# Two layers on a graph in one kernel: the 2 KB vector `bm` is fetched from ACT's queue at the start

## The chip, the cores and the metric

The kernel runs on one core of one Trainium2 chip. The metric is the device time of one execution in microseconds (us), as a median over runs. The kernel before took 2413.67 us (three runs, 2409.06 to 2415.69).

A core has five engines, each with its own instruction stream that is worked through in order: PE (TensorE, matrix products), DVE (VectorE), ACT (ScalarE), POOL (GpSimd) and SP (SyncE, which only issues transfers here). ACT and POOL issue transfers too. An instruction that needs another engine's result, or a transfer's data, waits on a semaphore, and all that stands behind it on its engine waits as well.

## The reference

The input `x` is 32 batches of 512 channels (C) by 1024 nodes (N), in float32; `adj` is a 512 x 512 matrix. Two layers follow one another, each on a normalized input:

```python
h = relu(layernorm(x))                  # over the 1024 nodes of a row
q, k = wq . h, wk . h                   # one number a node
scores[m, n] = leaky(q[n] + k[m])       # slope 0.01 below zero
att = softmax(scores) over n
x = x + relu(adj @ (h @ att.T) + bm)    # bm: 512 numbers, one a channel
h = relu(layernorm(x))
x = x + (h.T @ (adj*adj)).T + bias      # bias: 1024 numbers, one a node
```

`bm` is added to each channel of the first layer's output before its relu.

## The kernel before, in words

**Work.** A batch is held as four tiles of 128 channels x 1024 nodes (`c` = 0 to 3). The N x N attention is never built: since a score is a sum of two numbers behind a leaky slope, the nodes are sorted by `q`, and each row of the softmax becomes a sum of a prefix and a suffix of the sorted values. So for each batch:

- `load` (line 301, SP) brings `x`; `stats` (314, 315, DVE), `norm` (319, ACT), `slopes` (323, 325, DVE) and `relu` (332, ACT) normalize it.
- `scores` (344, PE, copied by ACT in 349) gives `q` and `k`; they go to DRAM and come back broadcast to all partitions as `qrow` (351, 353, SP).
- `rank` (384 to 393, DVE) and `lower` (400, ACT) count for each node how many are smaller; `to_rows` (420 to 426, DVE) makes row numbers `idx` of it.
- `value` (447, PE) is `pv` = `h` times the transposed `adj` (`wmT`), copied to `v` by ACT in `spread` (454); `scatter` (459, 460, POOL) writes each node's row of `v` to its sorted place in a DRAM table `td`.
- `fetch` (477, SP) reads the sorted table back as `vs`, after all scatters of the batch have landed. `weights` (486, 489, ACT), `later` (497, 501, DVE), `totals` (509 to 514, PE and DVE) and `stationary` (520, POOL) make the masks `sm`; `scan` (530, PE) and `sums` (540 to 547, ACT and SP) build prefix and suffix sums and write them to `td`.
- `gather` (552, POOL), `excess`, `divide`, `weigh` (577) and `combine` (581, DVE) take each node's sums; `turn` (588 on PE, 590 on DVE) transposes them and adds them into the reloaded `x`. Here `nbm`, which is -`bm`, is used: max(value, -`bm`) plus the residual. `bm` itself is added later, in `finish` (603).
- the second layer: statistics again, `lift` (338, adds `bias`), `propagate` (595, PE, `pg`) and `finish`.

**Order.** All these steps are listed with a due time each (the tables `PLAN`, `FIRST` and `LAST`), sorted by it, and written out in that order. The order on each engine is therefore fixed by the program, and steps of several batches interleave; batches 0 to 4 at the start have times of their own.

**Around the change.** Ahead of the steps stand constants: `wq` and `wk` are begun on ACT's queue (lines 222 and 223), and ACT computes a first square root, `root` (227). The step `biases` has three instructions: the transfer of `bm` (257) and of `bias` (258) on SP, and `nbm` on DVE (259). The step `pads` clears a tile on DVE (263, 264) and writes it to two places of each of the five tables, 20 transfers on SP (267, 268). A pair's second transfer overlaps the first in one row of the table, and so waits until the first has landed.

On SP, in order: eight `x` loads and `adj`, then batch 0's `qd` and `qrow`, one load, the 20 pads, two loads, `bm`, `bias`, one load, the six transfers of batch 0's fetch, batch 1's `qd` and `qrow`. On DVE, in order: statistics of batches 0 and 1, the ranks of batch 0 (with the pads' clearing among them), `nbm`, a tile's statistics, batch 1's slopes, batch 0's factors. The first reader of `nbm` after that is batch 0's `turn`, at 225.6 us; `bm_sb` is first used in `finish`, at 283.7 us.

A transfer issued from SP or ACT takes the next of eight completion semaphores, in turn, and waits for the transfer that had it last.

Of the kernel before, what the change touches and what calls it, by code (L numbers as in the profile page):

```python
# [16 lines left out]
P = 128  # L17
# [140 lines left out]
def kernel(  # L158
# [32 lines left out]
    nc = tc.nc  # L191
# [34 lines left out]
    root = const.tile([P, 1], F32, name="root")  # L226
    nc.scalar.activation(root, eps_sb, AF.Sqrt)
    bm_sb = const.tile([P, NC], F32, name="bm_sb")
    nbm = const.tile([P, NC], F32, name="nbm")
    bias_sb = const.tile([P, N], F32, name="bias_sb")  # L230
    before = const.tile([P, P], F32, name="before")
# [22 lines left out]
        nc.gpsimd.tensor_tensor(wsq, s.adj, s.adj, ALU.mult)  # L254

    def biases(s):
        nc.sync.dma_start(bm_sb, bm.rearrange("(c p) -> p c", p=P))
        nc.sync.dma_start(bias_sb, bias.partition_broadcast(P))
        nc.vector.tensor_scalar(nbm, bm_sb, -1.0, None, ALU.mult)

# [365 lines left out]
    for b in range(B):  # L626
        s = Batch()
        s.b, s.pv, s.v, s.sm, s.pt, s.pg = b, {}, {}, {}, {}, {}
        s.x, s.idx, s.vs, s.vt, s.sc = {}, {}, [], [], []
        if b == 0:  # L630
            for f in (
                adjacency, turn_adjacency, square, biases, pads, compare_mask, masks,
            ):
                plan(s, f, f.__name__, args=((),))
        for f in (
            load, reload, lift, rank, lower, value, spread, scatter, to_rows, scan, sums, gather,
            weigh,
        ):
            plan(s, f, f.__name__)
        for f in (  # L640
            scores, columns, factors, from_rows, fetch, weights, later, totals, excess, divide,
        ):
            plan(s, f, f.__name__, args=((),))
        for l in range(2):
            plan(s, norm, f"norm{l}", l, args=((),))
            plan(s, slopes, f"slopes{l}", l, args=((),))
            plan(s, stats, f"stats{l}", l)
            plan(s, relu, f"relu{l}", l)
        for i in range(NH):
            plan(s, turn, f"turn{i}", i)  # L650
        plan(s, stationary, "stationary", args=((0,), (3,), (6,)))
        for f in (propagate, finish):
            plan(s, f, f.__name__, args=all_of(NC, range(NH)))
        plan(s, combine, "combine", args=all_of(NN, (1, 2)))
# [31 lines left out]
```

## Time and profile before

| | us |
|---|---|
| median of three runs | 2413.67 |
| the profiled execution | 2400.17 |
| its span, first to last instruction | 2398.5 |
| PE busy in the span | 2305.7 (96%) |
| DVE busy | 1936.4 (81%) |
| ACT busy | 1585.2 (66%) |
| POOL busy | 723.7 (30%) |
| PE busy in the first 130 us | 90.9 |
| PE busy from 400 to 1000 us | 600.0 |

How to read it: a profile is of one execution, so a sum made from it is set against that execution's time. PE's matrix products are pipelined, and a busy PE may still run at half clock; the granted clock is given by stretch, 1.00 being full. In a list of waits the columns are the instruction that waited, what it waited for, then us in total, the number of times, and the longest. In a list in order of time they are the start in us, the duration in us, engine, line, operation, what is written <- what is read, shapes, the number of instructions that were merged, and in brackets the idle time of the engine just before with what ended it. A row by stretch has from:to and its length, then for PE, weight loads, DVE, ACT and POOL the busy us and the number of instructions, then the granted clock, the busy share of the 16 DMA engines, and GB/s. `SPq` and `ACTq` stand for an engine that issues a transfer.

### The profile page before, as it was taken

Reading aid. Unit: us, or ns where it says so; the run is one execution under the profiler, and the core shown is the slowest. Engines: PE = TensorE matmul, PEld = TensorE weight load, DVE = VectorE, ACT = ScalarE, POOL = GpSimd, SP = SyncE. Lnnn points to the kernel's source line nnn. Section 1 sums busy time; section 2 is a strip of 40 time slices with the busy share of each in tenths; the row PEclk is TensorE's granted clock in tenths of the full one; section 3 lists DMA queues with packets and bytes.
Section 4 is the critical chain, followed back from the end, with each engine's and each line's share of the span. In section 5 each row is a group of like instructions: output and inputs, shape, how many; then the busy total and the mean of one; then the engine's idle time right before and its main releaser. Section 6 shows DMA issues by size and latency. Waiting matters only on the chain.

```text
span 2398.5 us, 28425 instructions
## 1 busy us (share of the span) xinstructions
PE 2305.7 (96%) x7632; PEld 1004.9 (42%) x7632; DVE 1936.4 (81%) x5008; ACT 1585.2 (66%) x2880; POOL 723.7 (30%) x973
## 2 busy tenths in 40 slices
PE   5787999999999999999999999999999999999897
PEld 2233344444444444444444444444444444444343
DVE  5548878888888888888888888888898888888775
ACT  3666677667766767776766776676777766667541
POOL 2213332323442232333233233223233324223210
PEclk9898999999999999999999999999999999999999
DMA  5679879988889988988988888898898897888972
GB/s 163 183 184 281 275 251 299 283 268 274 309 258 299 302 257 270 304 284 273 299 274 251 300 298 272 285 301 253 273 309 280 276 299 243 266 282 275 286 294 97
DMA packets 206916, 643.49 MB, mean 268 GB/s; under 512 B 29130, under 2 KB 29258, under 8 KB 206756
## 3 DMA queue, kind: packets, MB, share of 16 engines
q1 hardware_dynamic: 148356, 372.68, 53.5%
q0 software_dynamic: 57344, 268.99, 30.0%
q8 instruction: 62, 1.02, 0.2%
q14 instruction: 98, 0.80, 0.1%
q10 hardware_dynamic: 1056, 0.00, 0.0%
HBM read 429.94 MB, written 211.62 MB: 267 GB/s over the span
## 4 chain that ended last, share of the span: by engine, by line
PE 87%; DMA 6%; DVE 2%; ACT 2%; issue 1%; SPq 1%; POOL 1%; POOLq 0%; DVEq 0%; ACTq 0%
PE pg L595 35%; PE pv L447 34%; PE sc L530 12%; PE tr L588 4%; DMA vs<-td 2%; PE pq L344 2%; DVE g L581 1%; DMA td<-pad 1%; DMA x<-in_x_dram 1%; DMA g<-td,idg 1%; DMA qd<-qr 0%; POOL g L552 0%; ACT junk L400 0%; SPq L477 0%; ACT t L543 0%
## 5 line engine op out<-in xcount | busy, mean ns | idle before, releaser
L447 PE MATMUL pv<-wmT,x 128*128 128x512 f32 x2048 | 907.0, 598 | 20.0 <-ACT x L332 20.0
L595 PE MATMUL pg<-h,wsq 128*128 128x512 f32 x2048 | 913.3, 598 | 10.6 <-ACT h L332 10.6
L447 PEld LDWEIGHTS pv<-wmT,x 128*128 128x128 f32 x2048 | 382.5, 191 | 511.7 <-issue 437.4
L595 PEld LDWEIGHTS pg<-h,wsq 128*128 128x128 f32 x2048 | 379.1, 190 | 509.6 <-issue 467.7
L520 POOL TENSOR_TENSOR sm<-mask_a,wc 128x192 f32<-128x192 f32 x96 | 49.4, 515 | 1283.8 <-DVE wc L497 815.5
L530 PE MATMUL sc<-vs,sm 128*64 128x512 f32 x1152 | 322.8, 629 | 38.7 <-POOL sm L520 17.2
L581 DVE SCALAR_TENSOR_TENSOR g<-g,cf 128x512 f32<-128x512 f32 x512 | 347.7, 746 | 12.4 <-ACT g L577 12.4
L460 POOL DMA_INDIRECT td<-v,idx x256 | 292.3, 1142 | 146.8 <-POOL v L459 49.8
L400 ACT ACTIVATE junk<-qrow,qk 128x1024 bf16<-128x1024 f32 x256 | 294.4, 1150 | 6.9 <-DMA qrow<-qd 5.1
L552 POOL DMA_INDIRECT g<-td,idg x256 | 243.1, 950 | 143.3 <-issue 71.5
L540 ACT COPY vs<-sc 1x512 f32<-1x512 f32 x256 | 145.4, 568 | 185.9 <-PE sc L530 185.7
L590 DVE SCALAR_TENSOR_TENSOR y<-tr,nbm,y 128x512 f32<-128x512 f32 x256 | 174.4, 743 | 97.2 <-PE tr L588 80.5
L603 DVE SCALAR_TENSOR_TENSOR y<-pg,bm_sb,y 128x512 f32<-128x512 f32 x256 | 187.9, 739 | 45.7 <-PE pg L595 45.4
L543 ACT COPY t<-sc 128x512 f32<-128x512 f32 x288 | 168.0, 583 | 74.1 <-DMA td<-t 69.0
L389 DVE TENSOR_SCALAR_CACHE_REDUCE junk<-qrow,qk,cnt 128x896 bf16<-128x896 f32 (+6 forms) x224 | 180.3, 805 | 8.2
L384 DVE TENSOR_SCALAR_CACHE_REDUCE junk<-qrow,qk 128x128 bf16<-128x128 f32 (+6 forms) x224 | 165.5, 739 | 14.0 <-DMA qrow<-qd 9.2
L530 PEld LDWEIGHTS sc<-vs,sm 128*64 128x64 f32 x1152 | 77.3, 139 | 231.9 <-issue 90.4
L314 DVE BATCH_NORM_STATS2 st<-x 128x6 f32<-128x512 f32 x256 | 162.9, 677 | 10.5 <-DMA x<-in_x_dram 10.5
L577 ACT ACTIVATE g<-g,cf 128x512 f32<-128x512 f32 x256 | 163.5, 712 | 6.4 <-DVE cf L571 6.4
L332 ACT ACTIVATE x<-x,nmr,rstd 128x1024 f32<-128x1024 f32 x128 | 148.5, 1233 | 25.8 <-DVE nmr L325 25.4
L338 DVE TENSOR_TENSOR y<-y,bias_sb 128x1024 f32<-128x1024 f32 x128 | 154.5, 1225 | 8.4 <-ACT h L332 8.4
L314 DVE BATCH_NORM_STATS2 st<-y 128x6 f32<-128x512 f32 x256 | 159.0, 663 | 0.0
(109 smaller groups left out, 1931.3 us busy)
## 6 DMA issues: line engine op xcount, KB each, us to landing
vs<-td SPq DMA_DIRECT2D x192, 384.8 KB
td<-t SPq DMA_DIRECT2D x576, 128.2 KB
x<-in_x_dram SPq DMA_DIRECT2D x128, 512.0 KB
y<-in_x_dram SPq DMA_DIRECT2D x128, 512.0 KB
out_dram<-y SPq DMA_DIRECT2D x128, 512.0 KB
qrow<-qd SPq DMA_DIRECT2D x32, 512.0 KB
td<-v,idx POOLq DMA_INDIRECT x256, 7.2
g<-td,idg POOLq DMA_INDIRECT x256, 11.4
```

The lines of the kernel that those rows point to most:

```text
L314: nc.vector.bn_stats(st[:, i, :], s.x[c][:, ts(i, HALF)])
L389: nc.vector.tensor_scalar(junk[:, j * P :], s.qrow[:, j * P :], qc, first, ALU.is_lt, ALU.add, accum_out=s.cnt[:, 1, j : j + 1],)
L400: nc.scalar.activation(junk, s.qrow, AF.Sign, bias=s.qk[:, 1, j : j + 1], accum_out=s.sgn[:, j : j + 1])
L447: nc.tensor.matmul(pv, s.h[c][:, ts(j, P)], wmT[:, c, :], start=(c == 0), stop=(c == NC - 1))
L460: i = nc.gpsimd.indirect_dma_start(tds[s.b % TABLES][:, :], bass.IndirectOffsetOnAxis(ap=s.idx[j // 4][:, j % 4 : j % 4 + 1], axis=0), v[: ...
L530: nc.tensor.matmul(p[ts(k, HP), :], s.sm[i][k], s.vs[h][:, 0:C], start=True, stop=True)
L543: nc.scalar.copy(t[:, 0:C], p)
L552: nc.gpsimd.indirect_dma_start(s.g[:, j, :], None, tds[s.b % TABLES][0 : 3 * NB * HP, :].rearrange("(s k) w -> s (k w)", k=3), bass.Indire ...
L581: nc.vector.scalar_tensor_tensor(r, s.g[:, j, k * W : k * W + C], s.cf[:, k, j : j + 1], r, ALU.mult, ALU.add)
L590: nc.vector.scalar_tensor_tensor(xh, pt, nbm[:, o : o + 1], xh, ALU.max, ALU.add)
L595: nc.tensor.matmul(pg, wsq[:, r, ts(c, P)], s.h[r][:, ts(i, HALF)], start=(r == 0), stop=(r == NC - 1),)
L603: nc.vector.scalar_tensor_tensor(xh, s.pg.pop((c, i)), bm_sb[:, c : c + 1], xh, ALU.add, ALU.add)
```

## The change

The transfer of `bm` is taken out of the step `biases` and begun with the constants, on ACT's queue, behind `root`. Nothing else is changed: `biases` still begins `bias` on SP and computes `nbm` on DVE, at its place in the order.

```diff
     root = const.tile([P, 1], F32, name="root")
     nc.scalar.activation(root, eps_sb, AF.Sqrt)
     bm_sb = const.tile([P, NC], F32, name="bm_sb")
+    nc.scalar.dma_start(bm_sb, bm.rearrange("(c p) -> p c", p=P))
     nbm = const.tile([P, NC], F32, name="nbm")
...
     def biases(s):
-        nc.sync.dma_start(bm_sb, bm.rearrange("(c p) -> p c", p=P))
         nc.sync.dma_start(bias_sb, bias.partition_broadcast(P))
         nc.vector.tensor_scalar(nbm, bm_sb, -1.0, None, ALU.mult)
```

## The prediction

> **What bounds the kernel now.** The page comes first. TensorE (PE) is busy for 2305.7 of 2398.5 us, and the row of forty slices shows where it is not:
>
> ```profile
> PE   5787999999999999999999999999999999999897
> ```
>
> Only the first four slices (240 us) and the last two fall short. I then took the busy time by stretch: from 300 us to 2000 us PE is idle for 1.7 us in all. The steps' order is fixed, so the end can only move if PE's idle time in the ramp moves. The wait that the diff touches lies in that ramp. The view of all that touches `bm_sb`, then the waits between 46 and 90 us:
>
> ```profile
> L259 DVE TENSOR_SCALAR nbm<-bm_sb x1: 169/169/169, 66.4 to 66.4; 128x4 f32<-128x4 f32 x1
>   DMA bm_sb<-in_L_gnn_bm_dram: 19.7, 1
> ```
> ```profile
> POOL sm L520 <- DVE wc L497: 26.9, 1, 26.9
> PE pv L447 <- ACT x L332: 19.8, 1, 19.8
> DVE nbm L259 <- DMA bm_sb<-in_L_gnn_bm_dram: 19.7, 1, 19.7
> ```
>
> VectorE (DVE) stands 19.7 us at `nbm`. Behind it are batch 1's slopes, behind those its relu on ScalarE (ACT), and behind that PE, idle 19.8 us. The tempting forecast is that all this comes back. So I asked for the order of time just after, and what PE meets next:
>
> ```profile
> 78.13 0.55 SPq L351 DMA_DIRECT2D qd<-qr  x1
> 81.62 0.30 ACT L486 ACTIVATE w<-vs,nq 128x3 f32<-128x3 f32 x1 [2.04 <-DMA vs<-td]
> 81.71 1.28 DVE L314 BATCH_NORM_STATS2 st<-x 128x6 f32<-128x512 f32 x2
> 83.15 0.31 DVE L497 TENSOR_SCALAR wc<-w,ident 128x9 f32<-128x9 f32 x2
> 83.88 0.50 POOL L520 TENSOR_TENSOR sm<-mask_b,wc 128x192 f32<-128x192 f32 x1
> 84.88 1.08 PE L530 MATMUL sc<-vs,sm 128*64 128x512 f32 x4
> ```
>
> At 81.62 ACT is waiting for batch 0's fetch (`vs<-td`) from DRAM; its last part sets `w`, then `wc`, `sm`, and PE's first scan matmul. In PE's order only three `pv` groups, the scores and one transpose (69.60 to 84.95) stand between the stall and that scan. The fetch stands on SP behind the pads (34.02 to 60.28), and no part of it waits for `nbm`. It, not the stall, is the later of the two gates.
>
> **What the Trainium skill says.** "DMA: Bandwidth & Descriptors", section "Issuing engines are not separate DMA queues": a transfer begun from another engine runs on the same 16 DMA engines and interleaves; only issue time is saved. The same page, "Queues, rings and completion order": each DMA engine goes round the queue rows packet by packet. The trace agrees on the kind of packet: ACT's queue moved 1056 packets for two 2 KB vectors, one for each 4-byte element and 32 more; and it agrees that they share, since the big loads slow down while they run:
>
> ```profile
> 2.00:7.00 5.00, 0.00 (x0) 0.00 (x0) 1.99 (x5) 1.49 (x2) 0.68 (x3) 1.00 0.83 246
> 7.00:13.00 6.00, 1.47 (x7) 1.50 (x8) 2.66 (x7) 0.00 (x0) 0.00 (x0) 1.00 1.04 402
> 10.00:13.00 3.00, 1.47 (x7) 1.50 (x8) 0.51 (x3) 0.00 (x0) 0.00 (x0) 1.00 1.04 415
> 63.00:64.00 1.00, 0.00 (x0) 0.00 (x0) 0.00 (x0) 0.00 (x0) 0.00 (x0) 0.50 1.02 410
> 64.00:66.00 2.00, 0.00 (x0) 0.00 (x0) 0.00 (x0) 0.00 (x0) 0.00 (x0) 0.50 0.89 210
> ```
>
> The last number is GB/s. "TensorE: Matmul & The Clock Gate", section "What's actually happening": PE drops to half clock after an idle window of about 3.4 us and returns after a busy one. Here the granted clock (third from the end) agrees: 0.50 over 57 to 69 and still over 69 to 74, then 0.96:
>
> ```profile
> 57.00:69.00 12.00, 0.00 (x0) 0.00 (x0) 2.49 (x7) 0.69 (x1) 0.00 (x0) 0.50 0.76 230
> 69.00:74.00 5.00, 4.40 (x5) 1.63 (x6) 4.07 (x19) 4.97 (x6) 0.00 (x0) 0.50 1.07 213
> 74.00:78.00 4.00, 4.00 (x37) 1.61 (x36) 0.00 (x0) 0.73 (x2) 0.00 (x0) 0.96 1.07 221
> ```
>
> **The change, part by part.**
>
> Start, added: one transfer of some 528 packets on ACT's queue after `root` (3.65 us). ACT's issue, 0.5 us as for `wq` and `wk`, is free: ACT then stands idle until 14.26. But its packets come while the fourth load of batch 0 is awaited; DVE starts on it at 12.70 after 2.46 us of waiting, and everything up to the pads and the fetch hangs on that. Upper bound: 2 to 7 us moved 246 GB/s against 415, so two such transfers (and the ramp) cost 5 x (1 - 246/415) = 2.0 us, 1.0 each. Lower bound: 7 to 13 us, with the tail of `wk` in it, lost 6 x (1 - 402/415) = 0.2. A gain is excluded: packets are added ahead of the load. I take +0.6.
>
> Start, a new wait: SP's loads of batch 1 wait for `wq` and `wk` already (1.2 and 3.2 us in SP's waits; the last two issue at 6.55 and 10.06), so these transfers share completion semaphores in turn, and `bm` joins the turn. `wk` came 3.5 us after `wq`, so I put `bm` at 13.6, and the last load's issue there too. A load issued at 0.81 was in use at 4.98, so the third load of batch 1, now issued about 10.1, is there by 14.3 (used at 17.72) and the fourth by 17.8 (used at 22.63). What is queued behind on SP, `qd`, issues at 21.85. Cost nothing; without that cover at most 3.5 us.
>
> Middle, removed: SP's issue, 0.43 us plus a gap, 0.47. SP's next issues run without a wait up to the fetch at 63.27, but the data are limited by the DMA engines, so this alone is hidden. What counts is the packets: over 64 to 66 us the engines moved 210 GB/s against 410, so 2 x (1 - 210/410) = -0.98 us for the data behind. Fetch landing: +0.6 - 0.98 = -0.4, from 81.6 to 81.2.
>
> Middle, the stall: DVE goes through `nbm` at 46.76 + 0.6 = 47.4. The relu then waits for ACT's copy of the last `pv` (ends 50.45), so PE starts batch 1 at 50.45 + 0.6 + 1.3 = 52.4, 17.2 us earlier. Its 15.35 us of work are over by about 67, and it waits for the scan. In the new order the statistics at 81.71 are long done, so `wc` follows `w` (82.10 - 0.4) at 81.75, not 83.15: -1.4. The scan needs the second `sm`, done at 84.38 - 1.4 = 83.0, against PE's 84.95: -1.9. That is what is left of 19.7.
>
> After it: the clock. PE has now idled from 67 to 83, so it is cold at the scan and not at 69.60. The cold `pv` group took 6.20 us against 3.70 warm: +2.5. That price moves from a place where PE was to wait anyway to one where PE then works without a break until 103. PE: -1.9 + 2.5 = +0.6. DVE's `den`, 1.36 us behind the scan, now takes 2.7: 83.0 + 2.7 = 85.7, not 86.24, and `qrow` (begun at 81.47 when `qd` has landed, which lies behind the fetch now) moves by some -0.3; so batch 1's ranks begin 0.3 to 0.5 earlier, and with them its scatters. PE's +0.6 reaches SP through `td<-t` (113.75), where the next fetch had 0.4 us to wait; the fetch at 115.00 moves by -0.4 to +0.2. Sum at the end: 0 within 1 us. The profiled execution took 2400.17 us (1.7 outside its span), 13.5 under the median of the runs, 2413.67; I carry the difference, 0, over to the median: 2413.7.
>
> **The rivals.**
>
> 1. The gain goes through: the scan would be ready whenever PE is. PE gains 17.2 us: 2396.5. For it: 19.7 us on DVE and the chain that ended last, which runs through `bm_sb`. Against: ACT's 2.04 us wait for the fetch at 81.62. It needs a fetch 17 us earlier, and SP is at the pads until 60.28. 5 in 100.
>
> 2. The start slips by all of the 3.5 us that a transfer on ACT's queue took: fetch +2.5, scan +1.0, PE +3.5, ranks +2.3; 2416.5. Against: 402 GB/s was kept with small packets present. 8 in 100.
>
> 3. Slower: PE stays cold after the scan. Each us of work at half clock costs half a us, and 2.3 are covered (1.9 and the 0.4 at SP). It decides (over 7.2 us) from 19 us of half clock on. Such a stretch exists: 0.50 over 207.4 to 221 with PE busy 6.26 us of 13.6 and 0.51 to 228. With 20 us: +7.7, 2421.4. Against: behind the scan stand solid `pv` groups (PE busy 15.00 of 15 us from 88 on), and at 69.60 the clock was back in under 5 us. 5 in 100.
>
> **How the numbers follow.** Some 0.3% (7.2 us) is what a measurement of this kernel can tell from no change. The collapse has 80 in 100, with 2411 to 2416.5 as its own range (1 us of the sum and the spread of the runs, 2409 to 2415.7, on a median). Rival 1 is faster, rival 3 slower, rival 2 the same; 2 in 100 are left for what I don't see, and 2 on each side of the collapse for the runs' spread. Faster 0.07, same 0.86, slower 0.07. The range 2408 to 2419.5 takes in the collapse, rival 2 and the spread.
>
> **What would show it.** Right: no wait for `bm` on DVE; PE at batch 1's `pv` by about 52; PE idle some 16 us ahead of the first scan at about 83, with half clock to about 88; a fetch that lands within 1 us of 81.6; PE solid from 300 us as now. Wrong: a fetch landing many us earlier (rival 1), DVE's fourth statistics at 14 or later, not 12.70 (rival 2), half clock beyond 100 us (rival 3). The forecast fails if something outside the ramp moves, such as a DMA order that repeats in each batch; I find none, since from `bias` on the turn of the semaphores is as before.

## The result, and the profile after

| | before | after |
|---|---|---|
| median of 12 runs, us | 2414.10 | 2412.64 |
| lowest and highest, us | 2409.06, 2416.16 | 2408.20, 2417.45 |
| ratio, with its 95% interval | | 0.9999 [0.9989, 1.0008] |
| the profiled execution, us | 2400.17 | 2409.72 |
| its span, us | 2398.5 | 2408.0 |

No difference can be measured: the interval leaves room for 2.7 us of gain and 1.9 us of loss. A stall of 19.7 us is gone from VectorE, and the kernel is not measurably faster. (The ratio is estimated from all runs; it is not the quotient of the two medians.)

The two profiled executions differ by 9.6 us the other way. That says nothing of the change: 28 runs of the kernel before on one chip, made for the experiments below, lay between 2410.79 and 2423.97 us. What a profile can show is the order of events in the ramp.

The page of after, its row of slices for PE, then its row for ACT's DMA queue:

```profile
PE   6787899999999999999999999999999999999797
...
q10 hardware_dynamic: 1584, 0.01, 0.0%
```

The first slice is fuller by a digit, the fifth and the 38th are emptier by one. ACT's queue now moves 1584 packets, not 1056: the 528 of `bm`. The view of all that touches `bm_sb`, the two lines on the transfer and on `nbm` (fastest, median and slowest in ns, then first and last start):

```profile
L229 ACTq DMA_DIRECT2D bm_sb<-in_L_gnn_bm_dram x1: 463/463/463, 0.8 to 0.8; - x1
L259 DVE TENSOR_SCALAR nbm<-bm_sb x1: 160/160/160, 47.0 to 47.0; 128x4 f32<-128x4 f32 x1
```

`nbm` runs at 47.01 without a wait, instead of 66.44 after 19.68. The waits of after between 46 and 90 us (us in total, times, longest):

```profile
POOL sm L520 <- DVE wc L497: 25.2, 1, 25.2
ACT w L486 <- DMA vs<-td: 18.2, 3, 12.8
...
PE sc L530 <- POOL sm L520: 13.7, 1, 13.7
...
DVE wc L497 <- ACT w L486: 8.6, 1, 8.6
...
PE pv L447 <- ACT x L332: 3.9, 2, 2.4
```

PE's wait for the relu fell from 19.8 to 3.9 us, and one of 13.7 us stands in its place, at the first scan. Read upwards, the list is the chain that makes it: the scan waits for `sm`, `sm` for `wc`, `wc` for `w`, and `w` for batch 0's fetch, `vs<-td`. The same chain in order of time, each engine's own list of after:

```profile
53.85 2.26 PE L447 MATMUL pv<-wmT,x 128*128 128x512 f32 x4 [2.36 <-ACT x L332]
...
82.75 2.43 PE L530 MATMUL sc<-vs,sm 128*64 128x512 f32 x4 [13.71 <-POOL sm L520]
...
87.56 14.00 PE L447 MATMUL pv<-wmT,x 128*128 128x512 f32 x32
```
```profile
81.49 0.30 ACT L486 ACTIVATE w<-vs,nq 128x3 f32<-128x3 f32 x1 [2.59 <-DMA vs<-td]
```
```profile
81.83 0.42 DVE L497 TENSOR_SCALAR wc<-w,ident 128x9 f32<-128x9 f32 x2 [8.57 <-ACT w L486]
...
85.55 0.17 DVE L514 COPY den<-pd 128x9 f32<-128x9 f32 x1 [3.20 <-PE pd L510]
86.09 0.34 DVE L384 TENSOR_SCALAR_CACHE_REDUCE junk<-qrow,qk 128x128 bf16<-128x128 f32 x1 [0.37 <-DMA qrow<-qd]
```

PE starts batch 1 at 53.85 instead of 69.60, 15.75 us earlier. But the last part of the fetch reaches `w` at 81.49, where it was 81.62, and so the scan begins at 82.75, only 2.13 us earlier than at 84.88. The scan's first four matmuls take 2.43 us, not 1.08, because PE is cold; the clock by stretch shows it (third number from the end):

```profile
57.00:69.00 12.00, 11.36 (x54) 4.67 (x54) 0.67 (x2) 2.18 (x4) 0.00 (x0) 1.00 0.64 190
69.00:74.00 5.00, 0.04 (x1) 0.00 (x0) 2.42 (x8) 0.00 (x0) 0.00 (x0) 0.91 1.04 282
74.00:78.00 4.00, 0.00 (x0) 0.00 (x0) 0.00 (x0) 0.49 (x2) 0.00 (x0) 0.50 1.08 241
78.00:83.00 5.00, 0.25 (x1) 0.26 (x2) 0.52 (x3) 1.44 (x5) 0.85 (x2) 0.50 0.54 121
83.00:86.00 3.00, 2.67 (x13) 1.60 (x13) 0.17 (x1) 0.76 (x2) 1.22 (x4) 0.50 0.97 291
86.00:90.00 4.00, 4.00 (x10) 1.67 (x11) 3.73 (x11) 3.94 (x8) 0.00 (x0) 0.91 0.34 87
```

The work of 57 to 69 is now done at the full clock, and the half clock has moved to 74 to 86, after the idle stretch (0.04 us of PE work from 69 to 74, none from 74 to 78). PE's unbroken stretch starts at 87.56, where PE's list of before has it at 88.27: 0.7 us are left of 19.7.

```profile
88.27 14.00 PE L447 MATMUL pv<-wmT,x 128*128 128x512 f32 x32
```

That the fetch reaches `w` at the same time is the sum of two movements that cancel. SP's list of before, then of after:

```profile
60.33 1.08 SPq L301 DMA_DIRECT2D x<-in_x_dram  x2
...
63.27 4.64 SPq L477 DMA_DIRECT2D vs<-td  x6
```
```profile
62.81 1.07 SPq L301 DMA_DIRECT2D x<-in_x_dram  x2
...
65.15 3.96 SPq L477 DMA_DIRECT2D vs<-td  x6
```

From the first load behind the pads to `w` it is 21.3 us in before (60.33 to 81.62) and 18.7 in after (62.81 to 81.49). This stretch, with the fetch in it, became 2.6 us shorter, and the pads ended 2.5 us later. The pads' pace varies between executions of one kernel, as the last experiment shows. The stretch behind them varies less: a second profile of before has 21.8 us, and four more profiles with an early `bm`, these pads and nothing added ahead of the fetch (`bm_sp`, `a_dve10`, `a_square`, `a_warm`) have 18.2 to 18.9. So the fetch came 2.4 to 3.6 us nearer to the pads, and it is chance that this does not show in the landing. How much of it reaches the end, the timings, with their 2.7 us of room, do not show.

### The profile page after: what moved, and what is told of

Same layout as the page of the kernel before. It is cut to its first block, busy times and chain, and to the rows that moved or that the text cites. A ratio compares the mean times of both kernels' runs of the same rounds, so it can differ in the third digit from the quotient of the medians.

```text
span 2408.0 us, 28425 instructions
## 1 busy us (share of the span) xinstructions
PE 2307.4 (96%) x7632; PEld 1004.8 (42%) x7632; DVE 1941.3 (81%) x5008; ACT 1585.4 (66%) x2880; POOL 724.6 (30%) x973
## 3 DMA queue, kind: packets, MB, share of 16 engines
q10 hardware_dynamic: 1584, 0.01, 0.0%
## 4 chain that ended last, share of the span: by engine, by line
PE 86%; DMA 6%; DVE 3%; ACT 2%; issue 1%; SPq 1%; POOL 1%; POOLq 0%; DVEq 0%; ACTq 0%
PE pg L595 34%; PE pv L447 33%; PE sc L530 12%; PE tr L588 4%; DMA vs<-td 3%; PE pq L344 2%; DVE g L581 1%; DMA td<-pad 1%; DMA g<-td,idg 1%; DVE junk L389 0%; DMA out_dram<-y 0%; DMA x<-in_x_dram 0%; ACT junk L400 0%; DMA qd<-qr 0%; POOL g L552 0%
## 5 line engine op out<-in xcount | busy, mean ns | idle before, releaser
L384 DVE TENSOR_SCALAR_CACHE_REDUCE junk<-qrow,qk 128x128 bf16<-128x128 f32 (+6 forms) x224 | 165.5, 739 | 13.6 <-DMA qrow<-qd 8.8
L454 ACT COPY v<-pv 128x512 f32<-128x512 f32 x256 | 142.2, 580 | 21.6 <-PE pv L447 17.8
## 6 DMA issues: line engine op xcount, KB each, us to landing
vs<-td SPq DMA_DIRECT2D x192, 384.8 KB
```

## The experiments

Three theories were set against each other. **T1**: the wait for `bm` was a wait in front of a later gate, the fetch; that gate moved by a few us at most, so the stall only moved to the scan. **T2**: the scan is ready earlier, but PE comes to it cold, and the lost clock gives the gain back. **T3**: the ramp does not set the end at all, so nothing done in it could show. Ratios are to the kernel before on the same chip; the chips of the different sets gave it medians from 2414.1 to 2418.6 us.

### Moving the gate itself

The pads' second transfer of each pair waits for the first, since both write one row of the table. Without that row in the first transfer, nothing waits, the table's contents are the same, and SP gets to the fetch sooner.

```diff
-                nc.sync.dma_start(sorted_rows(td, 0, NB)[o, 0], pad[0:NB, :])
+                nc.sync.dma_start(sorted_rows(td, 0, NB - 1)[o, 0], pad[0 : NB - 1, :])
```

With this edit in the kernel after (`a_pads`), and in the kernel before, with `bm` still on SP's queue (`b_pads`):

> The changed kernel, and the first transfer of each pair of pads is one row shorter (8 of 9 rows), so that the pair no longer overlaps and the second need not wait for the first; what is written to the tables is the same. Theory 1 (batch 0's fetch, which stands behind the pads on SP, is the gate of the first scan, and the end moves with that scan): the pads take some 10 us of SP and not 28, the fetch is issued when the scatters have landed, at about 60 us and not 65, and with the loads ahead of it already done it lands at about 73 and not 81.5; the first scan starts at 74 to 76, not 82.75; ratio to the kernel before 0.9965 to 0.998. Theory 2 (PE's clock, cold after its wait, gave the gain back): the scan comes earlier but the end moves by less than 2 us, ratio 0.999 to 1.001. Theory 3 (the ramp does not set the end): scan earlier, ratio 1.000.

> The kernel before (bm on SP, behind the pads) with the same shorter pads. Theory 1: SP comes to bm at about 46 us, so it lands at about 50 and DVE's stall shrinks from 19.7 to some 4 us; the first scan at the same 74 to 76 us as in the changed kernel with shorter pads, and the same ratio within 0.1%: where bm stands is of no account, what stands ahead of the fetch is. If the place of bm mattered by itself, this one would end some 4 us later than its twin.

SP's waits from 20 to 70 us, first of after, then of `a_pads`:

```profile
SPq L268 <- DMA td<-pad: 18.1, 10, 3.1
```
```profile
SPq L477 <- DMA td<-v,idx: 11.6, 3, 10.3
```

The 18.1 us of waits among the pads are gone. SP is at the loads at 45.58 instead of 62.81, but the fetch starts at 60.37 and not 17 us earlier, because it now waits 10.3 us for the last scatters. Even so it lands early. PE's list of `a_pads`, then of `b_pads`:

```profile
54.05 6.04 PE L447 MATMUL pv<-wmT,x 128*128 128x512 f32 x8 [4.09 <-ACT x L332]
75.05 2.43 PE L530 MATMUL sc<-vs,sm 128*64 128x512 f32 x4 [5.80 <-POOL sm L520]
```
```profile
59.02 6.20 PE L447 MATMUL pv<-wmT,x 128*128 128x512 f32 x8 [7.15 <-ACT x L332]
75.55 1.11 PE L530 MATMUL sc<-vs,sm 128*64 128x512 f32 x3 [1.18 <-POOL sm L520]
```

| | third `w` | scan | median, us | before on that chip | ratio |
|---|---|---|---|---|---|
| `a_pads` | 73.79 | 75.05 | 2408.42 | 2418.64 | 0.9961 [0.9947, 0.9975] |
| `b_pads` | 74.29 | 75.55 | 2409.20 | 2418.64 | 0.9955 [0.9940, 0.9970] |

The fetch lands 7.7 us earlier than in after, the scan follows, and by the ratios 9.4 us (6.0 to 12.8) and 10.9 us (7.3 to 14.5) come off the end. With `bm` late or early, the same: in `b_pads` PE starts batch 1 five us later (DVE still waits 8.9 us for `bm`, where I had expected about 4), and the scan absorbs it. That is what T1 says: the gain belongs to whatever moves the fetch. T3 falls, since an earlier scan shows in the end, and T2's forecast for this run, less than 2 us, falls with it. One thing is not told apart: the edit also brings the loads behind the pads forward by 17 us, and their share in the gain was not tested alone.

### How much of PE's early start is worth nothing

If T1 is right, DVE can be held up at `nbm` again, by unused work, and nothing happens until the delay reaches the scan. 14 (`a_dve10`) and 43 (`a_dve30`) extra statistics into an unused tile:

```diff
         nc.sync.dma_start(bias_sb, bias.partition_broadcast(P))
+        extra = sp.tile([P, 6], F32, tag="extra", name="extra", bufs=1)
+        for _ in range(14):
+            nc.vector.bn_stats(extra, wmT[:, 0, :])
         nc.vector.tensor_scalar(nbm, bm_sb, -1.0, None, ALU.mult)
```

> The changed kernel with 14 additional statistics instructions on DVE just ahead of nbm (about 0.69 us each, 9.6 us in all; their result is used by nothing). Theory 1: PE starts batch 1 some 6 to 10 us later than 53.85 us, but the first scan stays at 82.75 within 0.5 us and the ratio at 1.000 within 0.1%: half of the stall is put back and costs nothing. If the removed stall had been worth its length, the end would move by 9.6 us, ratio 1.004.

> The same with 43 additional instructions (29.7 us). Theory 1: DVE is now later than the fetch: PE starts batch 1 at about 80 us and comes to the first scan at about 95, 12 us later than 82.75; the end moves by 10 to 13 us, ratio 1.004 to 1.0055, so that only what exceeds some 17 us of the 29.7 is paid for. Theory 3 (the ramp does not set the end): 1.000. If every us of DVE's stall counted: 1.012.

PE's list of `a_dve10`, then of `a_dve30`:

```profile
60.35 6.04 PE L450 MATMUL pv<-wmT,x 128*128 128x512 f32 x8 [10.18 <-ACT x L335]
81.85 2.43 PE L533 MATMUL sc<-vs,sm 128*64 128x512 f32 x4 [6.31 <-POOL sm L523]
```
```profile
81.27 3.38 PE L450 MATMUL pv<-wmT,x 128*128 128x512 f32 x4 [29.60 <-ACT x L335]
...
96.39 1.08 PE L533 MATMUL sc<-vs,sm 128*64 128x512 f32 x4
```

With 14, PE starts 6.5 us later than in after, the wait at the scan shrinks from 13.71 to 6.31, and the time is that of before: 2418.44 us, 1.0000 [0.9989, 1.0011]. With 43, PE starts 27.4 us later, the scan has no wait left and begins 13.6 us later than in after, and the end moves: 2428.74 us, 1.0041 [1.0027, 1.0055], that is 10.1 us (6.5 to 13.3 by the interval). The wait at the scan is slack up to its length, and cost beyond it.

### The other gates: scatters and the clock

Batch 0's scatters are what the fetch waits for once the pads are quick. POOL does a 3.61 us product (`square`) among them; moved to a later time in the plan, with the pads' edit (`a_pads_square`) and without it (`a_square`):

```diff
-    "square": (63.05,),
+    "square": (130.0,),
```

> The changed kernel with the shorter pads, and the 3.6 us product wsq on POOL moved from the midst of batch 0's scatters to a due time of 130. Theory 1, one step further: with the shorter pads the fetch (60.37 us) waits for the scatters and no longer for SP, so scatters that end 3.6 us earlier bring the fetch to about 57, its landing to about 70 and the first scan to 71 to 72, not 75.05; ratio to the kernel before lower by another 0.001 to 0.0015, 0.9945 to 0.995. If something else holds the fetch at 60, the scan stays at 75 and the ratio at 0.996. The slopes' second instruction on DVE, 3.85 us beside wsq, takes about 0.2 us.

> The changed kernel with only the product wsq moved to a due time of 130. Theory 1: the scatters end 3.6 us earlier, but the fetch stands behind the pads, so it is issued at 63 to 65 us and the first scan stays at 81.5 to 83.5; PE starts batch 1 at 52 to 53.5, not 53.85. If the scatters were the gate, the scan would come at 79.

`a_pads_square` missed: the last scatter is issued at 52.95 instead of 56.12, but the fetch starts at 60.39 as before, `w` is ready at 74.08 and the scan at 75.34; 2410.97 against 2417.80 us, 0.9963 [0.9949, 0.9978]. What holds the scatters' data is not POOL's issue. `a_square`, one run of 2418.04 us, starts PE at 51.76 and waits 15.55 us for `sm`: the scan is at 82.49, so the scatters are not the gate in the kernel after.

To take T2 by itself, 14 matmuls on data at hand, into an unused bank, keep PE busy just ahead of the first scan (`a_warm`):

```diff
+        if s.b == 0 and i == 0:
+            pw = bank("warm")
+            for n in range(14):
+                nc.tensor.matmul(pw, wmT[:, 0, 0:P], wmT[:, 1, :], start=(n == 0), stop=(n == 13))
```

> The changed kernel with 14 matrix products (into a bank of their own, read by nothing) on PE between the third pv group of batch 1 and the first scan, some 12.6 us in a wait of 13.7. The clock is then full at the scan: the scan group takes about 1.1 us, not 2.43, and den comes at 84.4, not 85.55, but the ranks of batch 1 begin at 86.0 as now, since qrow lands only then; PE's solid stretch begins at 86.3, not 87.56. Theory 2 (the cold clock holds the gain back): the ranks begin over 1 us earlier. Theory 1: within 0.5 us of 86.1.

PE's list of `a_warm` in order of time:

```profile
68.71 12.18 PE L531 MATMUL warm<-wmT 128*128 128x512 f32 x28
81.44 1.11 PE L534 MATMUL sc<-vs,sm 128*64 128x512 f32 x3 [0.54 <-POOL sm L520]
```

The scan is warm. (The 14 matmuls stand as 28 entries in the trace.) The pads happened to be 1.3 us quicker in this execution (`w` at 80.18), so I compare from the landing on: batch 1's ranks begin 4.32 us after `w` here, and 4.60 in after. A warm PE is worth 0.3 us to them, since they then wait 1.13 us for `qrow` instead; PE itself begins its unbroken stretch 5.07 us after `w` and not 6.07, 1.0 us better. The single run took 2412.99 us, inside the spread. T2 exists, at a size of 0.3 to 1 us; it is not where 17 us went.

### Sizes: small packets, and less data ahead of the fetch

Four unused copies of the transfer of `bm` on SP, ahead of `bias` (`a_dead4`):

```diff
+        for n in range(4):
+            dead = sp.tile([P, NC], F32, tag=f"dead{n}", name=f"dead{n}", bufs=1)
+            nc.sync.dma_start(dead, bm.rearrange("(c p) -> p c", p=P))
         nc.sync.dma_start(bias_sb, bias.partition_broadcast(P))
```

> The changed kernel with four transfers of bm (into tiles that nothing reads) on SP at the place where the one stood before, so the packets' cost without any wait for them. From 64 to 66 us of the kernel before I worked out 0.98 us for one: the fetch then lands 3.9 us later, the scan at 86.7, not 82.75, the end 3 to 4 us later, ratio 1.001 to 1.002. If only SP's issue counts (0.47 each): 1.9 us. If one cost 2 us, as the fetch's later issue and same landing in the changed kernel hint: 8 us and more, ratio 1.003.

`w` is at 84.30 and the scan at 85.55, 2.8 us later than in after. From the first load behind the pads (63.13) to `w` it is 21.2 us, 2.5 more than in after: 0.6 us for each 2 KB, not the 0.98 I had worked out. SP's issue is in that figure and is not told apart from the packets: the four take 2.08 us to issue, `bias` behind them 1.98 instead of 0.43, and the fetch is issued 4.0 us later than in after. The time, 2421.15 against 2417.80 us, 1.0009 [0.9996, 1.0022], goes the same way, but its interval holds 1.

`a_lean` takes `a_pads_square` and issues `bias` and one `x` load, 1 MB, behind the fetch instead of ahead of it:

```diff
-    "biases": (44.64,),
+    "biases": (71.6,),
...
+            if name == "load" and s.b == 3 and n == 0:
+                t = 71.5
```

> The changed kernel with shorter pads and wsq moved, and with two 512 KB transfers that nobody needs yet (bias, and the first load of batch 3) moved on SP from ahead of batch 0's fetch to behind batch 1's qrow; nbm stays on DVE one tile's statistics later and its bm is long there. The earlier scatters of the last kernel did not land earlier; if that is because their data shared the DMA engines with these loads, 1 MB less at some 400 GB/s is 2.5 us: scatters landed at 57 to 58, not 60.3, fetch landed at 71 to 72, not 74.1, first scan at 72 to 73.5, not 75.3; ratio 0.9950 to 0.9960. If the scatters land at 60 for another reason, the scan stays at 75 and the ratio at 0.9963.

The fetch starts at 58.76, 1.6 us earlier (I had expected 2.5 to 3), and the scan is at 73.61, 1.7 earlier. So part of what held the scatters' data is the loads that share the DMA engines. The end shows nothing more: 2409.43 against 2417.95 us, 0.9972 [0.9962, 0.9982], where I had forecast 0.9950 to 0.9960. Whether another gate comes next there is open.

### The stall with no early transfer at all

If the transfer's place doesn't matter, the kernel before can lose its stall by moving the step `biases`, `nbm` and all, to 88.0 in the plan (`b_late`):

```diff
-    "biases": (44.64,),
+    "biases": (88.0,),
```

> The kernel before with bm still on SP, but the whole step biases (both transfers and nbm) due at 88 and not 44.64: its transfers stand behind batch 1's qrow on SP, nbm between the fetch's wc and den on DVE. The stall at 46.8 us is gone by the order alone, and bm and bias no longer lie ahead of the fetch. Theory 1: PE starts batch 1 at 52 to 54 as in the changed kernel and waits at the first scan, which comes at 80 to 82 (half a MB less ahead of the fetch, about 1.5 us); nbm then waits some 2 to 4 us for bm, ahead of den, so the ranks of batch 1 begin at 86 to 88. Ratio 0.999 to 1.001. If a stall of 19.7 us that vanishes were worth something in itself: 0.993.

The list of DVE, then of PE, in `b_late`:

```profile
85.14 0.17 DVE L259 TENSOR_SCALAR nbm<-bm_sb 128x4 f32<-128x4 f32 x1 [4.94 <-DMA bm_sb<-in_L_gnn_bm_dram]
```
```profile
53.50 2.26 PE L447 MATMUL pv<-wmT,x 128*128 128x512 f32 x4 [2.01 <-ACT x L332]
...
80.60 2.43 PE L530 MATMUL sc<-vs,sm 128*64 128x512 f32 x4 [11.92 <-POOL sm L520]
```

PE's early start comes back with `bm` on SP, and again ends in a wait at the scan. 2414.11 against 2416.98 us, 0.9988 [0.9979, 0.9997]. The end is some 2.9 us earlier than before's (0.7 to 5.1 by the interval). That goes with the shorter way of the fetch: from the first load behind the pads (61.20) to `w` (79.35) it is 18.15 us here and 21.29 in before, with `bm` and the 512 KB of `bias` no longer ahead of it.

### Spread, and the place of the early transfer

Two last runs of one execution each: the kernel before once more, unchanged (`before_again`), and the kernel after with `bm` begun early on SP (`bm_sp`).

```diff
-    nc.scalar.dma_start(bm_sb, bm.rearrange("(c p) -> p c", p=P))
+    nc.sync.dma_start(bm_sb, bm.rearrange("(c p) -> p c", p=P))
```

> The kernel before, unchanged, for a second profile of it. In the first one the last pads were issued at 59.83 us and the fetch landed at 81.6; in the changed kernel at 62.32 and 81.5. If the later pads come from the change, this profile has them at 59.8 again; if they are the spread of executions, it has them anywhere from 59.8 to 62.5. The stall at nbm: 19 to 22 us, the first scan at 84.9 to 87, the span within 10 us of 2398.5.

> The changed kernel with bm begun at the same place in the program, but on SP's queue, ahead of the first load of x. The loads of batch 0 are issued 0.45 us later and have 528 small packets ahead of them in their own queue: DVE's statistics of the fourth tile begin at 13 to 13.8 us and not 12.80, all up to the scan moves by that, first scan at 83 to 84; the end is the same within 2 us of the changed kernel's runs (2408 to 2417).

`before_again` took 2422.69 us, with a span of 2421.0, 22.5 us over the first profile of the same kernel, where I had expected at most 10: `nbm` at 68.53 after 21.91 us, `w` at 84.32, the scan at 87.23. The last pad was issued at 61.99, where the first profile had 59.83 and after 62.32. From the first pad to the last it is 25.8 and 28.1 us in these two profiles of one kernel, and 26.6 to 28.5 in the seven profiles with an early `bm` and these pads. So the pads' pace in after, which looks like a loss of 2.5 us against before, lies in the spread of executions. `bm_sp`, 2415.59 us, has the fourth statistics at 13.10 (12.80 in after), PE at 54.47, `w` at 82.02 and the scan at 83.28, each of the last three about half a us later than in after. For the ramp either queue does.

## Why the prediction was right, by its own steps

**The collapse: right.** The later of the two gates was the fetch, as the list in order of time had it. Predicted: fetch at 81.2, scan at 83.0, PE idle some 16 us ahead of it, unbroken from some 0.6 us later than before. Measured: 81.49, 82.75, 13.71 us, and 0.7 earlier. `a_pads` and `b_pads` show that moving the fetch moves the end whatever is done with `bm`, `a_dve10` that 6.5 us of PE's early start are worth nothing that can be measured. Two slips of the reading changed nothing: PE's early work is over by 67.75 in the prediction's own sum, not 67 (it was over at 69.04), and at the end of the kernel it is the 38th and the 40th slice that fall short, not the last two.

**`bm` behind `root` at 3.65: wrong, without effect.** The constants stand outside the part of the program that fixes the order of the steps (`tc.manual_schedule()`). There the transfer, which depends on nothing, went ahead of three instructions that are written before it. ACT's list of after:

```profile
0.81 0.46 ACTq L229 DMA_DIRECT2D bm_sb<-in_L_gnn_bm_dram  x1
1.31 0.52 ACTq L222 DMA_DIRECT2D wqk<-in_L_gnn_wq_dram  x1
1.86 0.53 ACTq L223 DMA_DIRECT2D wqk<-in_L_gnn_wk_dram  x1
```

**The start slip of 0.6: mis-sized.** DVE's fourth statistics begin at 12.80 instead of 12.70: 0.1 us. Over all profiles it is 0.1 to 0.4: batch 0's `nmr`, just behind them, begins at 14.76 to 14.81 in the four with a late `bm`, and at 14.89 to 15.18 in the nine with an early one on ACT's queue. From 2 to 7 us the engines moved 277 GB/s (246 before), from 7 to 13 us 377 (402 before): 5 x 277 + 6 x 377 = 3647 against 5 x 246 + 6 x 402 = 3642 KB, so over both stretches no data were lost. With three small transfers instead of two, the first stretch even moved more. So its 246 GB/s, which the prediction reads as large loads slowed by small packets, does not show that: my upper bound priced the ramp of the first us as if the small packets had caused it.

**SP's wait for `bm`'s semaphore: right.** `bm` joined the turn, at its front and not at its end, so that the last load still waits for `wk`. SP's waits from 0 to 20 us in after:

```profile
SPq L301 <- DMA wqk<-in_L_gnn_wk_dram: 3.9, 1, 3.9
SPq L301 <- DMA wqk<-in_L_gnn_wq_dram: 3.6, 1, 3.6
SPq L301 <- DMA bm_sb<-in_L_gnn_bm_dram: 2.2, 1, 2.2
```

The last load is issued at 14.29 (predicted 13.6, before 10.06), and the statistics that need it run without a wait, so the cover held.

**PE at 52.4: 1.45 us late, for two reasons I hadn't seen.** Batch 1's relu stands on ACT behind the copy of batch 0's last `pv`, and waits for `nmr` from DVE. The list of ACT, of DVE, then of POOL, in after:

```profile
51.57 0.59 ACT L454 COPY v<-pv 128x512 f32<-128x512 f32 x1 [2.84 <-PE pv L447]
52.56 2.37 ACT L332 ACTIVATE x<-x,nmr,rstd 128x1024 f32<-128x1024 f32 x2 [0.40 <-DVE nmr L325]
```
```profile
48.67 3.85 DVE L325 SCALAR_TENSOR_TENSOR nmr<-mv,rstd 128x4 f32<-128x4 f32 x1
```
```profile
48.89 3.61 POOL L255 TENSOR_TENSOR wsq<-adjn 128x2048 f32<-128x2048 f32 x1
```

The copy ends at 52.16, where the prediction has 51.05: that is 1.1 of the 1.45 us. PE's `pv` groups of batch 0 took 29.0 us and not 27.6, at a granted clock of 0.64 over 17 to 22 us and 0.80 over 22 to 30, where before has 1.00 in both. This is not the change: the second profile of before has 0.69 and 0.77, and 29.3 us for the groups, while `a_pads` and `bm_sp` took 27.6.

The other 0.40 us is the wait for `nmr`, which takes 0.16 us for batch 0. Taken off its stall, DVE met POOL's `square`. Where batch 0's groups took 27.6 us (`a_pads`, `a_dead4`, `bm_sp`), ACT waits 1.8 to 2.3 us for it. None of this cost anything here, since PE had 13.71 us to wait. The Trainium skill says in "SBUF — State Buffer", section "SBUF: two separate sides", that a DVE operation with two SBUF inputs and a GpSimd operation that reads SBUF take a shared pair of ports as an exclusive lock: the one that starts first has it for the whole instruction, and the other blocks. The runs agree on the blocking: 3.85 to 3.92 us in the six profiles (after, `a_pads`, `a_warm`, `a_dead4`, `b_late`, `bm_sp`) where `square` runs at that time, and 0.16 where `square` was moved away (`a_square`, `a_pads_square`, `a_lean`) or `nmr` comes later (`b_pads`, `a_dve10`, `a_dve30`). They don't show who starts first: in the record it is `nmr`, by 0.22 us in after, and it is the one that blocks.

**The small packets' price: mis-sized, and not the whole.** I had 0.98 us for the removed transfer; `a_dead4` gives 0.6 for each, issue included. Yet without the one the way from the first load behind the pads to `w` is 2.4 to 3.6 us shorter, about as much as the four put on. That the landing moved by -0.13, near the -0.4 of the prediction, is luck: the pads ended later in after. About 0.9 us of the shorter way is a quicker fetch: while it has the DMA engines nearly to itself they moved 239 GB/s in after (72 to 79 us) and 219 in before (70 to 78), and it is 6 x 384.8 KB. With these pads, the seven profiles with an early `bm` have 232 to 251 GB/s there. The three with a late one have 217 to 219, and among them is `b_late`, where `bm` comes behind the fetch, so packets ahead of it are not the reason. PE is busy in some of either kind and idle in others. With the pads' edit all four profiles have 218 to 225. The cause is not settled.

**The cold clock at 2.5: mis-sized.** I took a whole cold `pv` group against a warm one. PE's lead of 2.13 us at the scan is 0.7 behind it, so the price was 1.4, of which 1.35 are the scan's first group (2.43 against 1.08). It also lies partly under waits that a warm PE would meet: `a_warm` gains only 0.3 for the ranks. Of what hangs on it, batch 1's ranks began 0.26 us earlier (predicted 0.3 to 0.5), and the next fetch was issued at 115.32, 0.3 us later (predicted -0.4 to +0.2).

**The rivals of the prediction.** The gain going through is excluded by the ratio; a start slip of 3.5 us by the 0.1; a PE cold beyond 100 us by the clock, which is 0.91 over 86 to 90 and 1.00 over 90 to 103.

**The sum.** 0 within 1 us; the ratio's interval, -2.7 to +1.9 us, holds it. The time of 2413.7 stood 1.1 us over the median. The errors of the single terms are smaller than what the timings can tell, and some cancel: the result bears out the collapse, not each price in the sum.

## What to carry to other kernels

Before pricing a removed wait, go from the waiting instruction to what its engine's consumers wait for next, and look up when that arrives: a wait is worth only the distance to the next gate, here 2.1 of 19.7 us. Then work on the later gate; here it was a one-row overlap between transfers to DRAM, and removing it made the kernel 0.4% faster with `bm` in either place. Moving an engine's work to an earlier time also moves it beside other engines' work, so look at what runs there.

## What the runs showed of the hardware

- A DVE operation on 128x4 numbers took 3.85 us, not 0.16, beside a POOL product of 3.61 us.
- Four element-wise transfers of 2 KB ahead of a large one delayed it by 2.5 us, 0.6 each with their issue; at the start of the kernel one more cost 0.1 to 0.4.
- The same 64 entries of PE work (batch 0's `pv`) took 27.6 us in some executions and 28.9 to 29.5 in others of the same and of other kernels. In before and after, which took 27.6 and 29.0, the granted clock over 17 to 30 us was 1.00 in the one, and 0.64 and then 0.80 in the other.
- Two profiles of one kernel had spans of 2398.5 and 2421.0 us, 22.5 apart. In the set of the first, 12 runs lay between 2409.06 and 2416.16 us, in that of the second 23 runs between 2411.87 and 2424.13.
